# Set-up of a four-layer image kernel: statistics and transposes by image halves, and a new order of its first products

## Chip, cores and metric

The kernel runs on one core of one Trainium2 chip. The metric is the device time of one execution in microseconds; lower is better. A core has TensorE (PE in the profile; PEld is its weight load), VectorE (DVE), ScalarE (ACT), GpSimd (POOL) and SyncE (SP). SP, ACT and POOL also issue DMA transfers, each from a queue of its own, in order.

## What is computed

The input is x, 1024 images of 16 x 16 positions x 16 channels, f32. Four residual blocks follow one another. Each normalises its input by group (mean and variance over two neighbouring channels and all positions of an image, eight groups, with a small number added to the variance), applies a layer, and adds the result to its input. The layers are: a linear map of the whole image (4096 to 4096), given as a tensor train of three cores

```python
for core in cores:
    r, o, i, k = core.shape
    res_t = res.reshape(bs, r, i, -1)
    new = jnp.einsum('roik,brix->bkox', core, res_t)
```

then a cellular-automaton step (a fixed 3 x 3 filter, two dense layers, an alive mask), a 3 x 3 convolution with 16 channels, and a second cellular-automaton step. Only the first block and a piece of weight preparation for the last are touched here.

## The kernel before

The images are worked on as two sets of 512 (n = 0, 1), and each set again as two halves of 256. Images lie in the free dimension, and features in partitions, so x must be transposed: in the file the images are rows.

**The first layer.** The train's cores are multiplied out into a matrix of blocks, and the product of matrix and images is made with a table of 13 products (OUTER) of combined matrix blocks with combined image blocks, and inside each of them with 7 products (INNER, L561) in the manner of Strassen's scheme. A phase is one entry of OUTER; it has 4 units (u, numbered through all phases), each of 7 products of 2 steps. A step is four matmuls of 128 x 128 by 128 x 256 into a half of one PSUM bank (`po`). The phases are run one after the other by `run` (L1987), which calls a phase's steps in order, and between them, at set shares of the phase, the items of background lists: (list, from, to).

Product k of a unit multiplies a matrix (`w11`, `w00`, `w01`, or a sum: `s1`, `s2`, `s5`, `s7`) with a block of images (X[b, t, n]: b half of lines, n image half) or a combination (E[0..2]):

```python
("s2", (0, 0), {(1, 0): 1, (1, 1): -1}),   ("s5", (1, 1), {(0, 1): 1, (0, 0): -1}),
("w11", (1, 0), {(0, 0): 1, (1, 0): 1}),   ("s1", 0, {(0, 0): 1, (1, 1): 1}),
("s7", 1, {(0, 0): 1}),   ("w01", 2, {(1, 1): 1}),   ("w00", (0, 1), {(0, 1): 1, (1, 1): 1}),
```

Around each step `pieces` (L1546) issues work for the same or the next unit: `build` (L1447: 16 or 32 row-tiled matmuls `pw<-R,gq` and four ScalarE copies make a quarter matrix w), `mix` (L1474, VectorE, sums of two blocks of w), `gload` (L1422, loads gq from the DRAM table g_dram), `gather` (L1597, adds po into the unit's result r), and `store` (L1510, writes r into xf in DRAM; where a block has been written before, by an accumulating DMA of POOL at L1541). Engines take their work in the order in which it is issued; a buffer is handed out again when its last reader is done.

**The set-up** (L2041–2092) is written out in order. `train_setup` (L608): `early` (L660) makes 64 products `pg` of two cores, copies them to gw with 16 ScalarE copies (L672), and `keep_g` (L648) writes them to g_dram: four DMAs at L651 to g_dram[0], eight at L658 to g_dram[1]. `rest` is 12 further such pieces (`piece`, L678), which are made in phase 0. `input_steps(0)` (L1063): eight 1 MB loads of x on SP (L1074), `stats` (L1086, bn_stats for 128 images and half their lines), `turn` (L1088, four 128 x 128 transposes and a copy of 512 columns, for one half line, 8 positions x 16 channels, and all 512 images), `aggregate` (L1116), `root` (L1118–1120), `newton` (L1124), `widen` (L1134, means or inverse deviations written out to 128 columns), `spread` (L1142, their transposes, copied into `mr`), `kept` (L1145, lines written to xr in DRAM). `first_normed` (L1176) and `centre_scale` (L1174) subtract the mean and multiply, for the blocks x00, x11, x10, x01 of phase 0; `combined` (L1187, work at L1203) makes the five combinations of blocks; `part_steps(j)` (L1217) makes the image blocks of phase j one phase ahead, which for j = 1 reads xr.

In before, statistics of all 512 images come first, then the first normed block, then phase 0. The half of the transposes that are lines 8–15 (`lines[1]`) run in phase 0 at 0.12–0.42, `part_steps(1)` at 0.43–0.99. The dictionary `before` lists what is issued ahead of which step of phase 0. `set3` (an item list of `nca_weights`, L228) prepares the last layer's weights in phase 7; its `store` (L328–330) writes them to DRAM from POOL, and `conv_weights` and `fold3`, after it, read them or reuse their room in the tile xn.

Of the kernel before, what the change touches and what calls it, by code (L numbers as in the profile page):

```python
# [13 lines left out]
AF = mybir.ActivationFunctionType  # L14
# [91 lines left out]
def conv_preact_kernel(ctx: ExitStack, tc: tile.TileContext, a: dict, out: bass.AP):  # L106
# [483 lines left out]
    def train_setup(room):  # L590
# [57 lines left out]
        def keep_g(h, q, g, queue):  # L648

            for w in range(2):  # L650
                queue.dma_start(  # L651
                    g_dram[0][h, q, w].rearrange("o s k (t f) -> (s k t) o f", t=2),
                    g[64 * w : 64 * w + 64],
                )
            for w in range(2):
                for v in range(2):
                    rows = slice(64 * w + 32 * v, 64 * w + 32 * v + 32)
                    queue.dma_start(  # L658
                        g_dram[1][v, q, w, :, h].rearrange("o k (t f) -> (k t) o f", t=2), g[rows]
                    )  # L660

        def early():

            g = work([P, 2, 8, P], "w0", "gw")
            pg = [bank([P, 2, 4, 64], "w", "pg") for _ in range(4)]
            for x in range(2):
                for k in range(4):
                    for r in range(4):
                        gmul(pg[r][:, x, k], 0, k % 2, x, r, k // 2)
            for q, x, r in product(range(2), range(2), range(4)):  # L670
                f = 64 * x + 16 * r
                A.copy(  # L672
                    g.rearrange("p q (o i) f -> p q i o f", i=2)[:, q, :, :, f : f + S],
                    pg[r][:, x, 2 * q : 2 * q + 2].rearrange("p i (o j) -> p i o j", j=S),
                )
                if (x, r) == (1, 3):
                    keep_g(0, q, g[:, q].rearrange("p (o i) f -> p o (i f)", i=2), G)
# [383 lines left out]
    def input_steps(n, tag, queue):  # L1061
# [4 lines left out]
        slots = flats[1 - n].rearrange("p (s f) -> p s f", s=8)  # L1066
        X = part_lines(0)

        def slot(half, bg):
            return slots[:, 0 if (n, half, bg) == (1, 1, 3) else 4 * half + bg]  # L1070

        def load(half, bg):
            b0 = n * NB + bg * P
            queue.dma_start(  # L1074
                slot(half, bg),
                a["x"][b0 : b0 + P, 8 * half : 8 * half + 8].rearrange("b h w c -> b (h w c)"),
            )
# [10 lines left out]
        def turn(h, wh):  # L1088
            pt = bank([P, 4, P], tag[h % len(tag)], "ptin")
            for bg in range(4):  # L1090
                x = slot(h // 8, bg).rearrange("p (h w f) -> p h w f", h=8, w=2)
                T.transpose(pt[:, bg], x[:, h % 8, wh], ident)
            pt = pt.rearrange("p g b -> p (g b)")
            if n == 0 and h < 8:
                if wh:
                    A.copy(X[:, 1, h], pt)
                else:
                    A.copy(raw[:, h], pt.rearrange("p (n i) -> p n i", n=2))
                return
            if h % 2 == 0:  # L1100
                st["l"] = work([P, 2, NB], "t4", "lines")
            A.copy(st["l"][:, h % 2], pt)
            if h % 2 == 1:
                nc.sync.dma_start(
                    xr[n][wh, h - 1 : h + 1].rearrange("h p b -> p h b"), st["l"]
                )
# [32 lines left out]
        def spread(k):  # L1139
            pt = bank([P, 4, P], tag[0], "ptmr")  # L1140
            for bg in range(4):
                T.transpose(pt[:, bg], st["e", k][:, bg], ident)  # L1142
            A.copy(mr[n][:, k], pt.rearrange("p g b -> p (g b)"))

        def kept(b):  # L1145
            to = xr[n][b, 0:8]
            if b:
                G.dma_start(to.rearrange("h p b -> p h b"), X[:, 1])
                return
            for i in range(2):  # L1150
                G.dma_start(
                    to.rearrange("h p (n b) -> p h n b", n=2)[:, :, i], raw[:, :, i]
                )
# [15 lines left out]
        return loads, stat, lines, tail, [lambda: spread(0), lambda: spread(1)], kept  # L1169
# [6 lines left out]
    def first_normed(b, i):  # L1176

        X, E = part_tile(0)
        cols = slice(256 * i, 256 * i + 256)

        def op(t, k):
            x = X[:, b, t : t + 4, i]
            centre_scale(x, x if b else raw[:, t : t + 4, i], 0, cols, k)

        return [(1.2, lambda t=t, k=k: op(t, k)) for t in (0, 4) for k in range(2)]
# [201 lines left out]
    def layer_train():  # L1387
# [59 lines left out]
        def build(u, h):  # L1447

            if u >= len(units):
                return  # L1450
            R, gs = st["R", units[u][0]], list(st["g", u, h].values())
            w = st["w", u, h] = work([P, 2, 2, 4, P], "w1" if h else "w0", "w")
            pw = [bank([P, 2, 2, P], "w", "pw") for _ in range(4)]
            for v in range(2):
                for i in range(2):
                    for k, g in enumerate(gs):
                        for r in range(4):
                            rows = slice(32 * r, 32 * r + 32)
                            T.matmul(  # L1459
                                pw[r][:, v, i], g[rows, P * (2 * v + i) : P * (2 * v + i) + P], R[rows, k],  # L1460
                                start=k == 0, stop=k == len(gs) - 1,
                            )
            for r in range(4):
                A.copy(  # L1464
                    w.rearrange("p b s t m -> p (b s t) m")[:, :, 32 * r : 32 * r + 32].rearrange(
                        "p k (v o) -> p v k o", v=2
                    ),
                    pw[r].rearrange("p v i (k o) -> p v (i k) o", o=S),
                )
# [4 lines left out]
        def mix(u, what):  # L1474
# [10 lines left out]
            into = block(u, 0, 1)  # L1485
            x, y = block(u, *x), block(u, *y)
            if out:
                t = st[what, u] = work([P, 2, 4, P], out, what)
                V.tensor_tensor(t.rearrange("p s t m -> p (s t m)"), x, y, f)  # L1489
            else:  # L1490
                V.tensor_tensor(into, x, y, f)
# [54 lines left out]
        def pieces(u, k):  # L1546

            ph, q = units[u]
            what, where, goes = INNER[k]

            def go(i):
                X, E = part_tile(ph)
                if i == 0:
                    at = {1: (1, 6144), 3: (1, 14336)}.get(u)
# [9 lines left out]
                po, at = st["po"], 2 * k + i  # L1564
# [3 lines left out]
                if at == 1 and u > 0:  # L1568
                    store(u - 1)
                if at == 2:  # L1570
                    mix(u, "s1")
                if at == 4:
                    mix(u, "s7")
# [6 lines left out]
                if at == 9:  # L1580
                    build(u + 1, 1)
                if at == 11:
                    gload(u + 2, 1)
                if at == 12:
                    mix(u + 1, "s2")
# [4 lines left out]
                if i == 1:  # L1590
                    gather(u, k, po, goes)
# [5 lines left out]
        def gather(u, k, po, goes):  # L1597
            r = st["r", u].rearrange("p s a (n i) -> p s (a n) i", n=2)
            at = {x: 2 * x[0] + x[1] for x in goes}
            if k in (2, 3, 6):  # L1600
# [4 lines left out]
            for x, sign in goes.items():  # L1605
                out = r[:, :, at[x]]
                if all(x not in INNER[j][2] for j in range(k)):
# [6 lines left out]

        steps = [
            [x for u in range(4 * ph, 4 * ph + 4) for k in range(7) for x in pieces(u, k)]
            for ph in range(NP)
        ]
# [421 lines left out]
    with ExitStack() as es:  # L2040
        stage(es, dict(t4=4, s=2, n=2, w1=1, w0=2, s2=1, s5=1, r=1, gq=2, R=2, A=1), dict(w=4, m=1, o=3))  # L2041
        sums, cores, early, rest = train_setup(flats[0][:, 8192:9216])
        tag = ["w"]
        loads, stat, lines, tail, (spread0, spread1), kept = input_steps(0, tag, nc.sync)
        now(loads)
# [3 lines left out]
        now([sums])  # L2049
        coefs(0)  # L2050
        now([cores] + stat[0])
        early()
        gload(0, 1, queue=G)
        gload(0, 0, queue=G)
        now(lines[0])
        kept(0)
        kept(1)
        gload(1, 0)
        gload(1, 1)
        build(0, 1)  # L2060
        build(0, 0)
        now(stat[1] + tail[:2])
        mix(0, "s2")
        now([spread0] + tail[2:] + [spread1])
        x00, x11, x10, x01 = (first_normed(*at) for at in ((0, 0), (1, 1), (1, 0), (0, 1)))
        now(x00[0::2] + x00[1::2])
        mix(0, "s5")
        now(x11[:2])
        tag[0] = "m"
        more = combined(0)  # L2070
        before = {
            1: x11[2:] + rest[0][0:1],
            2: x10 + rest[0][1:2] + more[0:2],
            4: more[2:4],
            5: more[4:6],
            7: x01,
            8: more[6:8],
            9: more[8:10],
        }
        free = (12, 15, 18, 22, 26, 29, 32, 36, 40, 43)  # L2080
        for i, piece in zip(free, rest[0][2:] + rest[1]):
            before[i] = [piece]
# [12 lines left out]
        for j in late:  # L2095
            sums_late(j)
        run(
            steps_of(phases[0]), 107, (), (lines[1], 0.12, 0.42), (part_steps(1), 0.43, 0.99),
        )
        tag.append("w")  # L2100
        loads, stat, lines, tail, more, _ = input_steps(1, tag, G)
# [4 lines left out]
        for i in range(4):  # L2106
# [9 lines left out]
            7: (set3, 0.85),  # L2116
# [85 lines left out]
```

## Time and profile before

| | us |
|---|---|
| median of 3 runs | 2743.33 |
| lowest and highest run | 2742.66, 2747.08 |
| the profiled execution's own time | 2746.07 |
| its span (first to last instruction) | 2744.3 |
| the fourth and the eighth load of x landed | 17.3, 30.6 |
| first product of phase 0 starts | 47.14 |
| last product of phase 0 ends | 182.95 |
| last product of phase 7 ends | 982.8 |

Mean granted TensorE clock: 0.991 of full speed.

How to read the profile: a row of the timeline is a start, a length, an engine, a line, what it writes and reads, how often, and in brackets how long the engine was idle ahead of it and whose work ended that. A row of the windows is a stretch from:to, its length, busy time (and number of instructions) of each engine, the granted TensorE clock, the busy share of the DMA engines and their GB/s. A row of the waits is an engine and what it works on, what it waited for, the total, how often, and the longest. PE busy says that matmuls were under way, not that they ran at full clock. Matmul durations overlap with their neighbours' by a little, so a rate (80 matmul records in 17.46 us) is safer than a mean.

### The profile page before, as it was taken

How to read it: one execution, taken by the hardware profiler on the slowest of the kernel's cores; microseconds unless marked ns; L12 is line 12 of the kernel's file. 1: busy time of each engine (PE TensorE's matmuls, PEld its weight loads, DVE VectorE, ACT ScalarE, POOL GpSimd, SP SyncE). 2: the span in 40 equal slices, each digit the busy share in tenths (PEclk: the TensorE clock that was granted, in tenths of full speed). 3: DMA queues.
4: the chain of work that ended last, by engine and by line, in shares of the span. 5: the costliest groups of instructions: out<-in, count | busy, mean ns of one | idle time of the engine just before them, and what ended most of it. 6: DMA issues, size and time to landing. Idle time of an engine off the chain costs nothing.

```text
span 2744.3 us, 47734 instructions
## 1 busy us (share of the span) xinstructions
PE 2675.8 (98%) x19246; PEld 1756.9 (64%) x19246; DVE 1994.9 (73%) x2416; ACT 1241.4 (45%) x2091; POOL 541.3 (20%) x690
## 2 busy tenths in 40 slices
PE   6999999999999999999999999999999999999997
PEld 5888888888888878888778733333333333334344
DVE  8597667867787766667887777658778858756654
ACT  3324222222232222333332276776767756676664
POOL 2000351312122742311331111111113221110000
PEclk8999999999999999999999999999999999999998
DMA  7686788997897687889689764555575866444665
GB/s 254 215 317 227 242 169 214 236 221 188 193 242 193 154 187 180 226 229 263 171 188 257 148 165 102 108 159 122 106 195 83 202 150 143 101 89 116 180 175 209
DMA packets 264796, 502.17 MB, mean 183 GB/s; under 512 B 32804, under 2 KB 100440, under 8 KB 255360
## 3 DMA queue, kind: packets, MB, share of 16 engines
q1 hardware_dynamic: 180752, 338.78, 37.1%
q0 software_dynamic: 83632, 160.22, 33.9%
q8 instruction: 152, 2.49, 0.4%
q14 instruction: 68, 0.56, 0.1%
q10 hardware_dynamic: 192, 0.13, 0.0%
HBM read 280.66 MB, written 223.35 MB: 184 GB/s over the span
## 4 chain that ended last, share of the span: by engine, by line
PE 81%; DVE 8%; DMA 5%; issue 3%; POOL 1%; ACT 1%; SPq 0%; DVEq 0%; POOLq 0%; ACTq 0%
PE po L1567 37%; PE ph L1974 21%; PE po L1803 8%; PE po L1658 5%; PE pw L1459 4%; DMA xn<-in_x_dram 1%; PE po L1667 1%; DVE xn L1174 1%; DMA xf<-r 1%; DMA xn<-xf 1%; DVE xn L1203 1%; PE ptx L1867 1%; DMA L_conv_kp<-xn 1%; DMA xb<-xn 0%; DMA xn<-xn 0%
## 5 line engine op out<-in xcount | busy, mean ns | idle before, releaser
L1977 ACT ACTIVATE hid<-ph,pack 128x512 f32<-128x512 f32 (+1 forms) x1040 | 641.3, 684 | 313.5 <-PE ph L1974 254.3
L1567 PE MATMUL po<-xn,s 128*128 128x256 f32 x3328 | 756.7, 384 | 13.6 <-DVE s L1489 7.2
L1567 PEld LDWEIGHTS po<-xn,s 128*128 128x128 f32 x3328 | 628.5, 191 | 117.5 <-issue 16.7
L1567 PE MATMUL po<-xn,w 128*128 128x256 f32 x2496 | 565.0, 381 | 1.4 <-DVE xn L1203 1.4
L1974 PE MATMUL ph<-xn,wq 32*128 32x512 f32 (+1 forms) x3752 | 518.3, 590 | 1.9 <-DVE u L1815 1.5
L1567 PEld LDWEIGHTS po<-xn,w 128*128 128x128 f32 x2496 | 468.2, 190 | 74.1 <-issue 5.9
L1464 ACT COPY w<-pw 128x512 f32<-128x512 f32 x416 | 213.6, 600 | 454.6 <-PE pw L1459 371.8
L1974 PEld LDWEIGHTS ph<-xn,wq 32*128 32x128 f32 x3752 | 233.6, 184 | 228.9 <-issue 210.0
L1974 PE MATMUL ph<-xn,pack 32*128 32x512 f32 x1288 | 274.2, 607 | 5.6 <-DVE u L1815 1.6
L1489 DVE TENSOR_TENSOR s<-w 128x1024 f32<-128x1024 f32 x208 | 251.2, 1217 | 28.1 <-PE po L1567 24.8
L1803 PE MATMUL po<-hid,pack 128*32 128x512 f32 (+1 forms) x2080 | 256.0, 592 | 0.8 <-ACT hid L1977 0.5
L1815 DVE SCALAR_TENSOR_TENSOR u<-po,pack,xn 128x512 f32<-128x512 f32 (+1 forms) x130 | 96.3, 741 | 168.2 <-PE po L1803 167.1
L1857 POOL DMA_DIRECT2D xf<-u x96 | 82.6, 860 | 618.7 <-DVE u L1855 592.1
L754 DVE TENSOR_TENSOR xn<-xn,m 128x1024 f32<-128x1024 f32 x128 | 150.2, 1217 | 34.7 <-ACT m L777 34.6
L1974 PEld LDWEIGHTS ph<-xn,pack 32*128 32x128 f32 x1288 | 115.6, 184 | 90.7 <-issue 63.1
L1803 PEld LDWEIGHTS po<-hid,pack 128*32 128x32 f32 x2080 | 53.9, 109 | 174.9 <-ACT hid L1977 86.3
L1658 PE MATMUL po<-xn,convw 128*128 128x512 f32 x368 | 163.6, 598 | 0.0
L1203 DVE TENSOR_TENSOR xn<-xn 128x1024 f32<-128x1024 f32 x130 | 152.7, 1215 | 8.0 <-DMA L_conv_kp<-xn 8.0
L1459 PE MATMUL pw<-R,gq 32*128 32x128 f32 x3328 | 143.7, 286 | 7.5 <-DVE small L1116 6.9
L1603 DVE TENSOR_TENSOR r<-r,po 128x1024 f32<-128x1024 f32 x78 | 95.0, 1218 | 72.9 <-PE po L1567 61.0
L1459 PEld LDWEIGHTS pw<-R,gq 32*128 32x128 f32 x3328 | 116.2, 188 | 41.9 <-issue 38.6
L1541 POOL DMA_DIRECT2D xf<-xn x69 | 89.8, 1776 | 251.2 <-DVE xn L1534 71.7
(229 smaller groups left out, 2784.9 us busy)
## 6 DMA issues: line engine op xcount, KB each, us to landing
xn<-xf SPq DMA_DIRECT2D x128, 512.0 KB
xn<-xb SPq DMA_DIRECT2D x36, 1024.0 KB
wq<-L_conv_wy SPq DMA_DIRECT2D x192, 192.0 KB
xf<-xn POOLq DMA_DIRECT2D x69, 512.0 KB, 10.8
piece<-xb SPq DMA_DIRECT2D x64, 512.0 KB
xf<-r POOLq DMA_DIRECT2D x48, 512.0 KB, 12.7
xf<-u POOLq DMA_DIRECT2D x96, 256.0 KB, 4.2
gq<-g_dram SPq DMA_DIRECT2D x94, 256.0 KB
```

The lines of the kernel that those rows point to most:

```text
L754: V.tensor_tensor(part, part, m().unsqueeze(1).broadcast_to([P, 2, NB]), op)
L1203: V.tensor_tensor(out, y, z, f)
L1459: T.matmul(pw[r][:, v, i], g[rows, P * (2 * v + i) : P * (2 * v + i) + P], R[rows, k], start=k == 0, stop=k == len(gs) - 1,)
L1464: A.copy(w.rearrange("p b s t m -> p (b s t) m")[:, :, 32 * r : 32 * r + 32].rearrange("p k (v o) -> p v k o", v=2), pw[r].rearrange("p v ...
L1489: V.tensor_tensor(t.rearrange("p s t m -> p (s t m)"), x, y, f)
L1567: T.matmul(po[:, i], matrix(u, what)[:, i, t], x, start=t == 0, stop=t == 3)
L1603: V.tensor_tensor(part, part, po.unsqueeze(2).broadcast_to([P, 2, 2, 256]), ALU.add)
L1658: T.matmul(st["po", h][wh], conv["fw"][:, y], X[:, 16 * wh + h + y - 1], start=y == max(0, 1 - h), stop=y == min(2, S - h),)
L1803: T.matmul(po[32 * j : 32 * j + 32], nca["w1"][:, v], hid[j], start=v == 0, stop=v == 1)
L1815: V.scalar_tensor_tensor(u, po, nca["b1"], X[:, 8 * q + w2, cols(hf)], ALU.add, ALU.add)
L1974: T.matmul(ph, w, x, start=k == 0, stop=k == len(tiles) - 1)
L1977: A.activation(h, ph, AF.Relu, bias=nca["bt"][:, r : r + 1])
```

## The change

- **Loads and statistics by halves.** `first_images` takes the place of `input_steps(0)`. SP loads images 0–255 (four loads of 1 MB); the other four loads are issued from POOL, two after the first g_dram writes and gq loads, two after the second g_dram writes. Statistics, root, Newton step, widening and spreading are done for 256 images at a time. A `turn` now takes two half lines of 256 images, again four transposes and one copy; its PSUM banks alternate between two tags.
- **The transposes.** In the set-up: all lines of images 0–255. In phase 0: all lines of images 256–511, in groups of 16 ahead of steps 4, 6 and 8. Their number is the same.
- **`early`** issues the copies and the g_dram[0] writes of q = 0 first, then `gload(0, 1)` and `gload(0, 0)`, then q = 1; the g_dram[1] writes come last on POOL.
- **Order of phase 0.** Products s2 and w11 of units 0 and 1, which need only images 0–255, come first; then the others. `build(1, 1)` and `mix(1, "s2")` move ahead, into other rooms; `gather` asks which results have been made rather than for fixed numbers.
- **Work ahead of the steps** (`before`): statistics of images 256–511, their root, widening and spreading, x11 and two pieces stand ahead of step 8, the first that needs them; x01 ahead of step 12.
- **Background of phase 0:** no `lines[1]`; `part_steps(1)` at 0.3–0.99 (0.43–0.99 before).
- **`set3`** in phase 7 ends at 0.75 of it (0.85 before).

```diff
-        loads, stat, lines, tail, (spread0, spread1), kept = input_steps(0, tag, nc.sync)
-        now(loads)
+        load, stats, turns, aggregate, root, newton, widen, spread = first_images(tag)
+        for bg in range(2):
+            load(0, bg)
+            load(1, bg)
...
-        now([cores] + stat[0])
-        early()
-        gload(0, 1, queue=G)
-        gload(0, 0, queue=G)
-        now(lines[0])
...
+        def first_g():
+            gload(0, 1, queue=G)
+            gload(0, 0, queue=G)
+            load(0, 2, G)
+            load(1, 2, G)
+
+        early((first_g, lambda: (load(0, 3, G), load(1, 3, G))))
+        stats(0, 1)
+        stats(1, 1)
+        aggregate(0)
+        aggregate(1)
+        now(turns(0, 0, 0))
+        root(0)
+        widen(0, 0)
+        newton(0)
+        widen(1, 0)
+        spread(0, 0)
+        part = turns(0, 0, 1)
+        now(part[:2])
+        spread(1, 0)
+        now(part[2:])
...
+        now(x00[0::2] + x00[1::2])
         build(0, 1)
         build(0, 0)
+        gload(1, 1)
+        gload(1, 0)
+        now(x10[0::2])
         mix(0, "s2")
+        now(x10[1::2] + more[0:2])
+        now(turns(1, 0, 0) + turns(1, 0, 1))
+        half1 = turns(1, 1, 0) + turns(1, 1, 1)
+        rest = rest[0] + rest[1]
         before = {
-            1: x11[2:] + rest[0][0:1],
-            2: x10 + rest[0][1:2] + more[0:2],
-            4: more[2:4],
-            5: more[4:6],
-            7: x01,
-            8: more[6:8],
-            9: more[8:10],
+            2: [lambda: build(1, 1)],
+            3: [lambda: stats(0, 2), lambda: mix(1, "s2")],
+            4: turns(0, 1, 0),
+            5: [lambda: stats(1, 2)],
+            6: turns(0, 1, 1),
+            7: [lambda: stats(0, 3), lambda: mix(0, "s5")],
+            8: [lambda: stats(1, 3), lambda: aggregate(2), lambda: aggregate(3)]
+            + half1[:4] + [lambda: root(1), lambda: widen(0, 1)]
+            + [lambda: newton(1), lambda: widen(1, 1), lambda: spread(0, 1), lambda: spread(1, 1)]
+            + rest[:2] + half1[4:] + x11[0::2] + x11[1::2],
+            9: more[2:4],
+            11: more[4:6],
+            12: x01[0::2] + x01[1::2],
+            13: more[6:8] + rest[2:3],
+            15: more[8:10] + rest[3:4],
         }
...
+            if ph == 0:
+                us = [(0, 0), (0, 2), (1, 0), (1, 2)] + [x for x in us if x[0] > 1 or x[1] not in (0, 2)]
...
-            steps_of(phases[0]), 107, (), (lines[1], 0.12, 0.42), (part_steps(1), 0.43, 0.99),
-        )
+        run(steps_of(phases[0]), 107, (), (part_steps(1), 0.3, 0.99))
...
-            7: (set3, 0.85),
+            7: (set3, 0.75),
```

The new routines, cut to what differs:

```python
def turn(half, i, wh, h):
    tag.append(tag.pop(0))
    pt = bank([P, 2, 2, P], tag[0], "ptin")
    for l, g in product(range(2), range(2)):
        x = slot(half, 2 * i + g).rearrange("p (h w f) -> p h w f", h=8, w=2)
        T.transpose(pt[:, l, g], x[:, h + l, wh], ident)
...
def root(i):
    gs = slice(2 * i, 2 * i + 2)
    V.tensor_scalar(st["ve"][:, gs], st["mv"][:, gs, :, 1], GN_EPS, None, ALU.add)
    A.activation(st["t"][:, gs], st["ve"][:, gs], AF.Sqrt)
...
def keep_g(h, q, g, queue, first=True, second=True):
    for w in range(2 * first):
        queue.dma_start(g_dram[0][h, q, w]...)
```

## Prediction

> **What bounds the kernel now.** I read the page's busy shares first, then the busy time of each engine by stretch (set-up, phase 0, the boundary to phase 1), then the timeline of the set-up, the clock in single 3.3 us stretches, and the waits around the two places where TensorE stands still.
>
> ```profile
> span 2744.3 us, 47734 instructions
> ...
> PE 2675.8 (98%) x19246; PEld 1756.9 (64%) x19246; DVE 1994.9 (73%) x2416; ACT 1241.4 (45%) x2091; POOL 541.3 (20%) x690
> ```
>
> TensorE is busy for 98%, so only its idle time (68 us) and its time at half clock can be won. By stretch (start:end, length, then busy time of PE, PEld, DVE, ACT, POOL, clock, DMA share, GB/s):
>
> ```profile
> 0.00:47.14 47.14, 24.17 (x211) 21.71 (x211) 37.13 (x143) 19.71 (x49) 15.37 (x30) 0.81 0.91 342
> 47.14:182.95 135.81, 134.16 (x960) 112.63 (x960) 104.53 (x97) 43.33 (x112) 0.56 (x1) 0.96 0.64 213
> 182.95:190.00 7.05, 4.25 (x13) 3.44 (x13) 7.05 (x7) 0.00 (x0) 3.16 (x6) 0.76 1.02 312
> ```
>
> The set-up holds a third of all idle time: 23 of 47 us. Phase 0 has none to speak of. At its end TensorE stands 2.8 us while VectorE is busy through the whole stretch. The set-up's path is seen in the timeline (start, length, engine, line, what, [idle before <- releaser]):
>
> ```profile
> 30.60 2.71 DVE L1086 BATCH_NORM_STATS2 bn<-xn 128x6 f32<-128x256 f32 x8
> 33.67 2.09 PE L1459 MATMUL pw<-R,gq 32*128 32x128 f32 x32 [6.89 <-DVE small L1116]
> 43.05 0.63 DVE L1134 COPY wide<-small 128x128 f32<-128x128 f32 x4
> 43.60 4.62 DVE L1174 TENSOR_TENSOR xn<-xn 128x1024 f32<-128x1024 f32 x4
> 47.14 3.78 PE L1567 MATMUL po<-xn,s 128*128 128x256 f32 x8 [2.63 <-DVE xn L1174]
> ```
>
> The last 1 MB of x lands at 30.6, its statistics follow, then root, Newton step, spreading and the first normed block: 16.5 us from landing to the first product. The clock (PE busy, clock, DMA share, GB/s):
>
> ```profile
> 29.50:32.80 3.30, 0.00 (x0) 0.50 0.91 332
> 46.60:49.90 3.30, 2.76 (x7) 0.50 0.04 14
> 50.00:53.30 3.30, 3.30 (x20) 0.50 0.00 0
> 53.40:56.70 3.30, 3.30 (x10) 0.50 0.00 0
> 56.80:60.20 3.40, 3.40 (x28) 1.00 0.08 18
> 183.10:186.40 3.30, 0.65 (x3) 1.00 1.04 288
> 186.50:189.90 3.40, 3.40 (x10) 0.50 0.99 330
> ```
>
> The idle set-up costs twice: the products from 47.1 to 56.8 run at half clock, 9.6 us for 4.8 us of work. The boundary wait does the same to 186.5–189.9: 1.7 us. Last, phase 8, where set3's weight stores are in the way:
>
> ```profile
> DVE xn L1203 <- DMA L_conv_kp<-xn: 8.0, 1, 8.0
> ACT xn L1609 <- DMA xf<-xn: 16.1, 1, 16.1
> ```
>
> **Part 1, the first product comes earlier.** Images 0–255 need four of the eight loads; in before the fourth landed at 17.3. Their last statistics then end near 20.3 (8 of them 2.7, with a short queue). Two aggregates of 0.69 to 21.7, root 0.3, half a widening 0.3, Newton 1.3, half a widening 0.3: 24.0, against 43.7 in before. The first normed block (4 x 1.16) is done at 28.7. So statistics are no longer late; the block matrices are. The first eight copies of gw follow half the products, so the first two g_dram writes are issued about 2 us before the 15.17 of before. There they took 8.6 us and more beside the x loads; now the loads are in by 17.3, so I put their landing at 20, and that of the gq load, 4.2 us in before, at 24.5. In before it was queued behind all writes, on GpSimd, until 29.03. From there the steps of before count (pw 2.1 cold, four copies, the second build, the mix 1.2): 32.9 for the second build. After it TensorE's order has 32 transposes for lines 8–15, which ScalarE empties in eight copies: 7.4 us at the cold 0.85 per four. First product at 40.2, so **6.9 us earlier**. Bounds: 36 if the transposes are warm, 47 if the gq load is as late as now. The half-clock products go too, since transposes fill the two windows ahead; I keep 0.5 of the 4.8, **4.3 less**.
>
> Queues: the eight g_dram[1] writes go last on GpSimd, behind four loads, but the first pair of lines that reads them, (0,1), comes in phase 2. The xr writes go from GpSimd (37.4–47.9 in before) to SP behind unit 1's gq loads, at some 0.6 each; only part_steps(1) reads them, from 0.30 of the phase on. Bounds 0 to 1; I take nothing.
>
> A page of the Trainium skill speaks against another piece: "DMA: Bandwidth & Descriptors", Issuing engines are not separate DMA queues, says that transfers from any engine end on the same 16 DMA engines. The g_dram writes that took 8.6–12.4 us beside loads at 420 GB/s, against 2.5–3.7 later alone, agree; by the page the four loads on GpSimd's queue win nothing by themselves, and their gain here is only that they start behind the gq loads.
>
> **Part 2, phase 0's own work** does not change: 56 steps of 1.746 (80 matmul records in 17.46), 8 builds of 1.1, 12 pieces of 1.1, 64 transposes at 0.6 per four: 129.4 us, which is before's 135.81 without 1.65 idle and 4.8 half clock. Half the transposes are still in the phase, those of images 256–511.
>
> **Part 3, two new waits.** The first four products (steps 0–7: 14.0, with a build and 32 transposes, 5.9, among them) last to about 60.8. In the whole phase I add 1.8 for pieces that take up to 1.24 and for transposes that wait for one of two banks. Then every further product needs x11 or x01, and these need statistics that are started only here: on VectorE behind the last gather 0.65, eight bn_stats 2.65, aggregates 1.4, root 0.3 and ScalarE's square root 0.3, widening 0.3, Newton 1.3, and x11's four operations 4.6: 11.7 us with the short waits between. Behind it in TensorE's queue stand 32 transposes, two pieces and small ones, 6.1 us. The wait is thus 6.0 us warm; but 4.5 of it lie in one piece, more than the 2.80 that made the clock half at 183, and the pieces ran in 1.97 instead of 1.1 and the transposes at 0.85 instead of 0.44 per four when cold, so I add 3.1: **9.1 us**. Bounds: 6.0 (no cold window) and 19 (rival 2). The second wait is ahead of the product of (0,5): VectorE has x01 (4.6), two more sums, mixes s7 and w01 and a gather in front, I count **2.9** (0 to 5).
>
> The page "TensorE: Matmul & The Clock Gate", Part 1, What's actually happening, has full speed back after one busy window of about 3.4 us. Products ran without a gap from 47.14 and were half until 56.8, with a run of sixteen 16-row matmuls in the window 50.0–53.3, so the row gives longer than the page; an estimate by the page puts the cold part at 1.7 instead of 3.1.
>
> Sum of phase 0: 40.2 + 0.5 + 129.4 + 1.8 + 9.1 + 2.9 = 183.9, against 182.95. Phase 0 ends **1.0 later**: what the set-up wins, the middle gives back.
>
> **Part 4, the boundary.** The second half of phase 0 held, in VectorE, 28.7 us per unit of 26.6 us: that is why it is busy from 136 to 185.75 but for 4 us, and the mix s is late. With part_steps(1) over 0.30–0.99 instead of 0.43–0.99, its share (about 18 of the 28.7) falls by 0.81, to 25.3 per unit. So the 2.8 idle and 1.7 half clock, **4.5 less**. Bounds: 0 (its gathers come behind x01's work, and VectorE is still behind) and 4.5. The line transposes that were spread over 0.12–0.42 are gone from there, so this stretch is lighter for TensorE as well, and nothing else is late.
>
> **Part 5, set3 at 0.75.** The store L328–L330 goes ahead of the unit's accumulating writes instead of behind them. In before kp was issued at 980.7 and landed at 998.2, and L1203 waited 8.0; TensorE stood 2.5 + 0.8 + 0.4 + 0.6. Earlier it lands near 986, before its reader (989). But those writes then queue behind L328, which waits for copies landing about 974, and land near 997 instead of 993.8; ScalarE's copy into that buffer already waited 16.1 for them, and TensorE follows. I take 4.3 won and 2.8 given back, **1.5 less**; bounds 4 more and 5 less.
>
> Sum: +1.0 (phase 0) - 4.5 - 1.5 = -5.0. Against the profiled execution's 2746.07 (span 2744.3) that is 2741.1. This execution lay 2.7 above the median of the runs, so I forecast 2743.33 - 5.0 = 2738.3. About 0.2% (5.5 us) is what a measurement of this kernel can tell from no change, so the forecast lies on the edge of "the same": 2737.8 is the bound.
>
> **Rivals.**
> 1. *The wait in the middle stays warm or set3's stall goes wholly.* The 4.5 us idle may be split over two windows (2.37 in one piece at 1364 made the clock half, 2.53 at 997 did not). Then 3.1 or 2.8 or both come back: 2733 to 2735. For it: the transposes lie in the first part of the wait. Against it: 2.80 was enough at 183.
> 2. *Slower: the clock stays half after the wait.* Steps 8 to 17 run with pieces and VectorE waits among them, as the window 50.0–53.3 did, and no window is filled with wide matmuls until about 101. Eight steps (14), a build and two pieces at half clock cost 13 more less the 2.9 that the second wait then hides: +10.3, 2748.6, and up to 2752. It decides where the first full window after the wait is cold beyond 75. Against it: from 52.75 on a window of products alone set it free.
> 3. *Nothing is won at the ends.* The gq load is late behind x loads, so the first product starts past 43, or VectorE is as far behind at the boundary and 4.5 stays: 2742 to 2746. For it: VectorE gets statistics and x11 into phase 0 that were in the set-up. Against it: up to 136 VectorE had room, with 27 us idle at waits for products, where it now works.
>
> **How the numbers follow.** Forecast 0.50 (2736 to 2742), rival 1 0.22, rival 2 0.10, rival 3 0.18. A little under half of the forecast's own case and nearly all of rival 1 lie below 2737.8: faster 0.45. Rival 2's upper part and a little of rival 3 lie above 2748.8: slower 0.09. The rest, 0.46, is the same. The range takes in rival 1's better end and rival 3, with rival 2's lower part left out: 2731 to 2747.
>
> **What would show it.** The first product of L1567 near 40; the second widening of images 0–255 ended near 24; no half clock in the first products; a stretch near 61–73 with a half clock and TensorE released by VectorE's wide and x11 operations; a wait of some 3 us ahead of (0,5) near 90–100; phase 0's last product near 184 and no wait behind it; kp landing near 986 without a VectorE wait, and ScalarE's wait for xf<-xn ending near 997. It is wrong if the first product starts later than 43, if the middle wait passes 12, or if VectorE is busy without a gap over the boundary.

## The result, and the profile after

The changed kernel takes 2751.72 us (median of 10 runs, 2749.01 to 2757.93) against 2743.45 (10 runs, 2741.40 to 2751.22): ratio 1.0029, 95% interval 1.0020 to 1.0039. It is slower by 8 us, where 5 us faster was forecast. The profiled execution took 2749.45 (span 2747.7), in the lower part of its runs, and that of before 2746.07, in the upper part of its own; so the two traces are only 3.4 us apart, and the experiments have to say which of the waits vary. One execution of a_xract, below, ran at a granted clock of 0.847 throughout (3088.77 us); its ratio leaves it out, and its row of phase 0 is from a second profile.

The page's first lines of after: the same number of matmuls, and TensorE's share is the same but for rounding (97.5% in both).

```profile
span 2747.7 us, 47757 instructions
...
PE 2678.5 (97%) x19246; PEld 1759.4 (64%) x19246; DVE 1995.6 (73%) x2424; ACT 1242.3 (45%) x2094; POOL 527.4 (19%) x691
```

Set-up, phase 0 in four parts, and the first 7 us of phase 1:

```profile
0.00:38.32 38.32, 25.35 (x207) 21.57 (x208) 34.48 (x105) 18.76 (x48) 14.37 (x30) 0.91 0.86 313
38.32:63.86 25.54, 20.91 (x132) 17.69 (x131) 8.64 (x21) 9.74 (x19) 0.55 (x1) 0.93 0.67 227
63.86:76.00 12.14, 7.52 (x61) 6.36 (x58) 11.26 (x40) 5.60 (x17) 0.00 (x0) 0.76 0.36 122
76.00:100.00 24.00, 19.42 (x112) 15.53 (x111) 16.41 (x16) 5.21 (x13) 0.00 (x0) 0.84 0.35 99
100.00:193.00 93.00, 91.69 (x674) 77.06 (x673) 75.13 (x73) 24.21 (x69) 1.17 (x3) 1.00 0.79 263
193.00:200.00 7.00, 7.00 (x34) 6.17 (x33) 7.00 (x7) 2.09 (x4) 2.55 (x5) 1.00 1.01 387
```

The first product starts at 38.32, 8.8 us earlier. But the next 62 us hold 14 us of TensorE idle time (4.6 + 4.6 + 4.6), where before had 1.65 in all of phase 0, and they run in part at half clock (0.93, 0.76, 0.84). The waits, from TensorE's own timeline:

```profile
45.49 1.40 PE L1546 MATMUL pw<-R,gq 32*128 32x128 f32 x32 [3.55 <-DMA gq<-g_dram]
46.82 5.13 PE L1660 MATMUL po<-xn,w 128*128 128x256 f32 x16
...
69.41 0.46 PE L1157 MATMUL ptmr<-ident,wide 128*128 128x128 f32 x2 [3.29 <-DVE wide L1149]
70.91 0.69 PE L1157 MATMUL ptmr<-ident,wide 128*128 128x128 f32 x2 [1.04 <-DVE wide L1149]
71.53 2.89 PE L644 MATMUL pg<-cores,convw 16*128 16x64 f32 x32
74.36 3.80 PE L1102 MATMUL ptin<-ident,xn 128*128 128x128 f32 x16
77.95 4.85 PE L1660 MATMUL po<-xn,s 128*128 128x256 f32 x16
...
90.76 3.62 PE L1660 MATMUL po<-xn,s 128*128 128x256 f32 x8 [3.21 <-DVE xn L1286]
...
98.70 1.99 PE L1660 MATMUL po<-xn,w 128*128 128x256 f32 x8 [1.37 <-DVE xn L1286]
```

Each matmul of a product stands in the trace as two records, so eight records are a step and sixteen a product. Counted from 38.32, the wait at 45.49 is ahead of product (0,2) (unit 0, product 2), those at 69.41 and 70.91 ahead of (0,1), that at 90.76 ahead of (0,4), which needs the combination E[1] (E1 below), and that at 98.70 ahead of (0,5), which needs E[2].

Read the lengths beside the waits. Sixteen records take 3.62 us at full clock; behind the first wait they take 5.13, behind the second 4.85, and behind the third eight take 3.62 instead of 1.99. Each of these three waits is paid a second time in clock: 1.5, 1.2 and 1.6 us, and the pieces and transposes at 71.5 to 78 on top. The clock in single stretches (PE busy, clock, DMA share, GB/s):

```profile
67.00:70.40 3.40, 0.46 (x2) 0.97 0.72 249
70.40:73.80 3.40, 2.89 (x32) 0.50 0.00 0
73.80:77.20 3.40, 3.40 (x19) 0.50 0.15 33
77.20:80.60 3.40, 3.40 (x12) 0.53 0.94 244
80.60:84.00 3.40, 3.40 (x44) 1.00 1.02 317
```

Where the span went, by the end of each phase on TensorE (after less before): phase 0 ends 9.1 us later (192.0 against 183.0), phase 1 at +9.0, phase 6 at +8.8, phase 8 at +5.4, the span at +3.4. So the boundary to phase 1 gave nothing, set3 in phases 7 and 8 gave 3.4, and 2.0 more fell in later phases, which the change doesn't touch; from the end of phase 8 on the kernels below scatter by 4 us.

At the boundary the wait for `s` is gone, but at 206.82 TensorE waits 2.83 for the fourth load of images 512–1023, with a half clock behind it:

```profile
206.82 0.48 PE L1192 MATMUL ptin<-ident,xn 128*128 128x128 f32 x1 [2.83 <-DMA xn<-in_x_dram]
207.09 3.40 PE L1660 MATMUL po<-xn,s 128*128 128x256 f32 x8
```

### The profile page after: what moved, and what is told of

It is laid out like the page before. It is cut to its first block, busy times and chain, and to the rows that moved or that the text cites. A ratio compares the mean times of both kernels' runs of the same rounds, so it can differ in the third digit from the quotient of the medians.

```text
span 2747.7 us, 47757 instructions
## 1 busy us (share of the span) xinstructions
PE 2678.5 (97%) x19246; PEld 1759.4 (64%) x19246; DVE 1995.6 (73%) x2424; ACT 1242.3 (45%) x2094; POOL 527.4 (19%) x691
## 4 chain that ended last, share of the span: by engine, by line
PE 85%; DVE 7%; DMA 3%; issue 1%; ACT 1%; SPq 0%; POOL 0%; DVEq 0%; POOLq 0%; ACTq 0%
PE po L1660 41%; PE ph L2070 21%; PE po L1899 8%; PE po L1754 5%; PE pw L1546 5%; PE po L1763 1%; DMA xn<-xf 1%; DMA xn<-in_x_dram 1%; PE ptx L1963 1%; PE ptin L1192 1%; DVE u L1911 1%; DVE xn L1286 0%; PE pcnt L1939 0%; DMA xn<-in_L_conv_fc_w_dram 0%; DVE xn L757 0%
## 5 line engine op out<-in xcount | busy, mean ns | idle before, releaser
L1660 PE MATMUL po<-xn,s 128*128 128x256 f32 x3312 | 748.9, 383 | 8.3 <-DVE s L1579 5.1
## 6 DMA issues: line engine op xcount, KB each, us to landing
wq<-L_conv_wy SPq DMA_DIRECT2D x192, 192.0 KB
```

The source lines that it names most:

```text
L1660: T.matmul(po[:, i], matrix(u, what)[:, i, t], x, start=t == 0, stop=t == 3)
```

## The experiments

Medians and ratios against before, which ran beside each (2742.79 to 2744.45 in the three sets of runs); phase 0's first product and end from the profile (a_xract's from its second profile). After did not run beside the experiments, so a difference to its median can be off by about 1.5 us; the ratios are the safer comparison.

| kernel | median us | ratio, 95% | phase 0 |
|---|---|---|---|
| before | 2743.45 | | 47.1–183.0 |
| after | 2751.72 | 1.0029, 1.0020–1.0039 | 38.3–192.0 |
| b_set3 | 2743.14 | 0.9995, 0.9986–1.0004 | 47.0–184.5 |
| b_parts | 2742.84 | 0.9996, 0.9987–1.0005 | 47.1–183.9 |
| a_loads | 2753.05 | 1.0034, 1.0021–1.0047 | 38.0–195.7 |
| a_stats | 2745.52 | 1.0007, 0.9998–1.0016 | 36.8–188.5 |
| a_actq | 2748.41 | 1.0012, 1.0002–1.0021 | 41.7–194.0 |
| a_late1 | 2750.82 | 1.0025, 1.0015–1.0034 | 36.5–197.6 |
| a_stats_actq | 2741.30 | 0.9985, 0.9975–0.9995 | 42.0–184.2 |
| a_best | 2736.45 | 0.9965, 0.9953–0.9978 | 40.7–179.9 |
| a_xract | 2745.40 | 1.0006, 0.9997–1.0015 | 38.8–188.6 |
| a_best2 | 2731.19 | 0.9953, 0.9939–0.9967 | 38.0–175.4 |
| b_best | 2740.98 | 0.9992, 0.9982–1.0001 | 47.3–186.7 |

Theory A, from the profile of after: the loss is order, not work; unit 1's gq load is late, the chain of statistics starts too late, and the boundary's stall had covered another wait. The main rival: VectorE's work binds the first 100 us, and removing one wait only moves it.

**b_set3, set3 alone.**

```diff
-            7: (set3, 0.85),
+            7: (set3, 0.75),
```

> The kernel before with one number changed: set3 ends at 0.75 of phase 7 instead of 0.85. Theory A (the earlier store of L_conv_kp takes the 8.0 us VectorE wait out of phase 8 and nothing gives it back): phase 8 about 5 us shorter, phase 7 up to 2 us longer because its PE work on fc_w meets a load, in all 3 us faster than before, about 2740. Theory B (as forecast: the accumulating xf writes behind L328 land later and ScalarE's copy waits for them): phase 8 only 1.5 us shorter.

In the profile phase 8 is 5.1 shorter and phase 7 1.5 longer (a 1.39 us wait at L287, fc_w's transposes, which now come before their load), as theory A has it. L_conv_kp lands at 971.5, 972.4, well before its reader, and the accumulating writes at 974.7 to 981.5, earlier too: the whole list of set3 was moved up, not its last item alone, so nothing was given back. The timed runs show only 1.3 less, and the interval includes none and 3.8. The next experiment gives a likely reason.

**b_parts, the boundary alone.**

```diff
-            steps_of(phases[0]), 107, (), (lines[1], 0.12, 0.42), (part_steps(1), 0.43, 0.99),
+            steps_of(phases[0]), 107, (), (lines[1], 0.02, 0.29), (part_steps(1), 0.3, 0.99),
```

> The kernel before with lines 8-15 transposed at 0.02-0.29 of phase 0 and part_steps(1) at 0.30-0.99 (0.12-0.42 and 0.43-0.99 before). Theory A (the 2.8 us wait for s at the start of phase 1 hides a wait for the x loads of images 512-1023, which can start only when phase 0's buffers are free): the wait for s goes, a wait of 2 to 3 us for xn<-in_x_dram with a half clock after it comes in its place some 10 us later, 0 +- 1.5 us against before. Theory B (the forecast's): 2.8 idle and 1.7 at half clock go, 4.5 us faster.

Theory A held in where, less in how much. The wait for `s` at phase 1's start is gone, and TensorE waits here instead:

```profile
195.28 0.55 PE L1092 MATMUL ptin<-ident,xn 128*128 128x128 f32 x3
198.71 0.33 PE L1092 MATMUL ptin<-ident,xn 128*128 128x128 f32 x1 [2.88 <-DMA xn<-in_x_dram]
198.88 1.90 PE L1567 MATMUL po<-xn,s 128*128 128x256 f32 x8
```

The three transposes done and the fourth waiting are one group: it needs 128 images from each of four loads. The loads were issued from 182.46, when VectorE's last read of their room was done, and the fourth landed at 198.67. The eight matmuls behind it took 1.90: no half clock this time, and phase 1 is 1.9 shorter than before's. The median is 1.6 below before's, with an interval that includes none. In the same run phase 8 is 3.7 shorter although set3 was left alone: kp landed at 993.8 instead of 998.2, and VectorE waited 4.3 for it instead of 8.0. Phases 7 and 8 together took 220.5 us here without set3's edit and 220.5 in b_set3 with it, against 224.2 in the profile of before. So that profile caught the stall at a length that another trace doesn't show, and what the edit is worth in the median is not shown to differ from nothing.

**a_loads, GpSimd's loads of x behind the g_dram[0] writes.**

```diff
         def first_g():
             gload(0, 1, queue=G)
             gload(0, 0, queue=G)
-            load(0, 2, G)
-            load(1, 2, G)
 
-        early((first_g, lambda: (load(0, 3, G), load(1, 3, G))))
+        early((first_g, lambda: [load(half, bg, G) for bg in (2, 3) for half in range(2)]))
```

> The changed kernel with the four loads of images 256-511 behind the second pair of g_dram[0] writes on GpSimd's queue (two of them were ahead of it). Theory A (those writes land at 33.2 behind the loads, so the gq load of unit 1 starts at 33.3 and lands at 45.5 beside the loads): the gq load starts near 28 and lands before 42, the 3.55 us wait of L1546 and the half clock after it go, 4 to 5 us faster than the changed kernel. Theory B (the lateness is the bandwidth and goes to the loads instead): statistics of images 256-511 come later, the wait ahead of step 8 grows by as much, no change.

Theory A missed. B's "no change" came in time (1.0034 against 1.0029), but not for its reason: the wait ahead of step 8 was the same 3.29 and 1.04 us. g_dram[0] landed at 28.3, 5 us earlier, SP issued the first gq load at 28.35, and it landed later than in after. SP's queue, then TensorE:

```profile
19.51 7.36 SPq L1115 DMA_DIRECT2D xr<-xn  x2
28.35 3.70 SPq L1521 DMA_DIRECT2D gq<-g_dram  x2
```

```profile
48.67 2.09 PE L1546 MATMUL pw<-R,gq 32*128 32x128 f32 x32 [7.02 <-DMA gq<-g_dram]
```

A 256 KB load took 20 us, more than the 12.2 in after (33.29 to 45.5). Ahead of it in the same queue are two xr writes of 1 MB each, in rows of 1 KB, the second issued 1.9 us before it: the writes that the change moved from GpSimd's queue to SP's. That gave theory A2, order within SP's queue.

**a_stats, statistics of images 256–511 ahead of step 3.**

```diff
-            3: [lambda: stats(0, 2), lambda: mix(1, "s2")],
+            3: [lambda: stats(0, 2), lambda: stats(1, 2), lambda: stats(0, 3), lambda: stats(1, 3)]
+            + [lambda: aggregate(2), lambda: aggregate(3), lambda: root(1), lambda: widen(0, 1)]
+            + [lambda: mix(1, "s2"), lambda: newton(1), lambda: widen(1, 1)],
             4: turns(0, 1, 0),
-            5: [lambda: stats(1, 2)],
-            6: turns(0, 1, 1),
-            7: [lambda: stats(0, 3), lambda: mix(0, "s5")],
-            8: [lambda: stats(1, 3), lambda: aggregate(2), lambda: aggregate(3)]
-            + half1[:4] + [lambda: root(1), lambda: widen(0, 1)]
-            + [lambda: newton(1), lambda: widen(1, 1), lambda: spread(0, 1), lambda: spread(1, 1)]
-            + rest[:2] + half1[4:] + x11[0::2] + x11[1::2],
+            6: [lambda: spread(0, 1), lambda: spread(1, 1)] + turns(0, 1, 1),
+            7: [lambda: mix(0, "s5")],
+            8: x11[0::2] + x11[1::2] + half1[:4] + rest[:2] + half1[4:],
```

> The changed kernel with all statistics of images 256-511 up to the second widening ahead of step 3, their spreading ahead of step 6, x11 first in front of step 8. Theory A (the wait in the middle is the chain from bn_stats to mr that starts only at step 7's end): idle 3.3 + 1.0 us and the half clock from 70 to 80 go, about 8 us faster than the changed kernel. Theory B (VectorE's sum of work binds the first 100 us, and its order only decides where the wait is): the wait moves to steps 3 to 5 or to x01 ahead of step 12, at most 3 us faster.

6 us faster than after by the medians; in the profile steps 7 to 8 shrink from 14.1 us (63.86 to 77.95) to 6.4 (67.01 to 73.38), and the clock stays full there:

```profile
47.20 2.09 PE L1546 MATMUL pw<-R,gq 32*128 32x128 f32 x32 [6.80 <-DMA gq<-g_dram]
...
69.20 1.94 PE L644 MATMUL pg<-cores,convw 16*128 16x64 f32 x32
71.07 1.09 PE L1102 MATMUL ptin<-ident,xn 128*128 128x128 f32 x8
72.45 1.09 PE L1102 MATMUL ptin<-ident,xn 128*128 128x128 f32 x8 [0.28 <-ACT lines L1109]
73.38 2.97 PE L1660 MATMUL po<-xn,s 128*128 128x256 f32 x13
```

So the wait in the middle was the late start of the chain, and worth 7.7 us there: VectorE had room at 39 to 49. Part of it is lost again in the wait for gq, 6.80 in this run.

**a_actq, unit 1's gq loads on ScalarE's queue.**

```diff
-        gload(1, 1)
-        gload(1, 0)
+        gload(1, 1, queue=A)
+        gload(1, 0, queue=A)
```

> The changed kernel with the two gq loads of unit 1 on ScalarE's queue instead of SP's. In the run with the loads of x moved back these two were issued 5 us earlier, at 28.4 and 31.7, and PE still waited until 48.7. Theory A2 (they stand behind the two 1 MB xr writes, in rows of 1 KB, that the change put on SP's queue): on a queue of their own they land some 5 us after issue near 34, and the 3.55 us wait and the half clock after it go, 5 us faster than the changed kernel. Theory B (the DMA engines as a whole are full until 46, whatever queue): they land near 45 as before, no change.

A2 held: issued at 35.04, no earlier than in after, they were there when TensorE came at 45.26, without a wait and without a half clock: step 2 starts 4.7 us after step 0, in after 8.5. TensorE came late enough that its timeline alone can't tell A2 from B; the semaphores in the trace can: the first load landed at 41.8, 6.8 us after its issue, where B had it near 45. The gain of 3.3 us is below the 5 expected, because ScalarE's queue stood at the issue until g_dram landed (31.96 to 35.04); the engine was idle for 2.32 us ahead of its next copies, the half clock lasted to 41.5, and the first product came at 41.7.

**a_late1, the transposes of images 512–1023 later.**

```diff
-            steps_of(phases[1]), 107, (), ([(0, x) for x in loads[:7]] + [8] + woven_in + tail, 0.0, 0.76),
+            steps_of(phases[1]), 107, (), ([(0, x) for x in loads[:7]] + [14] + woven_in + tail, 0.0, 0.76),
```

> The changed kernel with the transposes of images 512-1023 begun 14 instead of 8 us into phase 1. Theory A (what is late at the boundary, once the wait for s is gone, is the fourth 1 MB load, which lands 3.4 us after its first transpose is due): the 2.83 us wait and the half clock after it go, 4 us faster than the changed kernel. Theory B: the wait comes back at the next group of transposes or as VectorE load at the end of phase 1, no change.

The wait and the half clock are gone and phase 1 is 2.9 shorter than before's (after: 0.1), so in the profile theory A held, at 2.8 instead of 4. The median moved by 0.9 only, inside the intervals, so the timed runs don't show the gain by themselves. This kernel's phase 0 is the same code as after's, and so a second sample of it: the wait for gq was 6.15 here instead of 3.55, and phase 0 ended at 197.6 instead of 192.0. After's own profile has the shortest of the four such waits in kernels that leave writes and loads on SP's queue (3.55, 6.15, 6.80, 7.02).

**a_stats_actq, both edits.**

> The changed kernel with both edits: all statistics of images 256-511 ahead of step 3, and unit 1's gq loads on ScalarE's queue. If A2 holds the two gains add, since the early statistics alone only made the wait for gq longer (6.8 instead of 3.55): phase 0 ends near 181 to 183, 5 us ahead of the run with early statistics alone. If B holds: as that run, 2745.5. If VectorE's order binds after that, the wait shows up ahead of (1,2) or at x01.

2741.30: the gains add, 10.4 us below after, and the kernel is now slightly faster than before (ratio 0.9985, interval to 0.9995). Phase 0 ends at 184.2, 4.3 ahead of a_stats. The rival, by which a removed wait only comes back, is left only with the 3.21 us at 81.10, the wait for E1.

**a_best: also x01 ahead of step 7 and the later transposes of phase 1.**

```diff
-            7: [lambda: mix(0, "s5")],
+            7: [lambda: mix(0, "s5")] + x01[0::2] + x01[1::2],
...
-            12: x01[0::2] + x01[1::2],
...
-            steps_of(phases[1]), 107, (), ([(0, x) for x in loads[:7]] + [8] + woven_in + tail, 0.0, 0.76),
+            steps_of(phases[1]), 107, (), ([(0, x) for x in loads[:7]] + [14] + woven_in + tail, 0.0, 0.76),
```

> Early statistics, unit 1's gq loads on ScalarE's queue, x01 ahead of step 7 (VectorE stood 10 us there in the run with early statistics), and the transposes of images 512-1023 begun 14 us into phase 1. By theory A with A2 the four waits of phase 0 and the one of phase 1 go: 5 for gq, 8 for the statistics, 6 for x01, 4 for the boundary, less 2 for a phase that VectorE then binds: some 15 to 20 us below the changed kernel, 2733 to 2736, faster than both. If VectorE's sum of work binds (rival), not below 2743.

2736.45, 15.3 below after, faster than both kernels and half a microsecond short of the expected range. Phase 0 ends at 179.9; the 3.21 us for E1 are still there, at 79.99.

**a_xract, the two xr writes on ScalarE's queue.** This undoes the suspected part and leaves the gq loads where they were.

```diff
-            nc.sync.dma_start(to.rearrange("h p b -> p h b"), x)
+            (A if h + i == 0 else nc.sync).dma_start(to.rearrange("h p b -> p h b"), x)
```

> The changed kernel with the two 1 MB xr writes of images 0-255, lines 0-7, on ScalarE's queue; the gq loads of unit 1 stay on SP's. This undoes the part of the change that put these writes ahead of the loads in one queue. Theory A2 (order within SP's queue): gq lands some 5 us after its issue at 33 to 35, the wait of L1546 and its half clock go, and the first product keeps its early start near 37 to 38, 4 to 6 us faster than the changed kernel. Rival (ScalarE's queue is served faster than SP's, whatever stands in it; the gain of the last such run was the queue): gq on SP is as late as before, no change.

> The same kernel as the last but one experiment (xr writes of lines 0-7 on ScalarE's queue), for a profile at full clock, the first one's clock having been 0.85 throughout. Theory A2: no wait of L1546 for gq, steps 0 to 7 in 22 us instead of 25.5, phase 0 ends 4 to 6 us earlier than the changed kernel's. Rival: the wait is there and the time came from elsewhere.

6.3 us below after by the medians; A2 held, and the rival, that ScalarE's queue is the faster one, fell. The profile shows SP's gq load issued at 34.55 (by its semaphore it landed at 41.5, 6.9 us later) and no wait:

```profile
38.79 3.62 PE L1660 MATMUL po<-xn,s 128*128 128x256 f32 x16
42.34 1.17 PE L1546 MATMUL pw<-R,gq 32*128 32x128 f32 x32
43.44 3.72 PE L1660 MATMUL po<-xn,w 128*128 128x256 f32 x16
```

Steps 0 to 7 took 20.3 us (38.8 to 59.1) against 25.5 in after. Phase 0 ends 3.4 us earlier than after's, less than the 4 to 6 expected: the half clock at the wait for E1 lasts from 84.5 to 94.8 here, in after from 90.7 to 94.1. The DMA packets in the traces show the order itself: in after the gq load's first packet moved at 41.5, 8.2 us after its issue and behind 1874 packets of 1 KB of the same queue; here at 38.1, 3.5 us after its issue, with none of them ahead in its queue.

**a_best2, a_best with the xr writes moved instead of the gq loads, and E1 earlier.**

```diff
-            9: more[2:4],
-            11: more[4:6],
+            9: more[2:6],
```

> Early statistics, x01 ahead of step 7, transposes of images 512-1023 14 us into phase 1, as in the fastest run so far; but with the xr writes on ScalarE's queue in place of the gq loads, and with the third combination E1 issued two steps earlier (the 3.2 us wait at 80.0 was for it). By theory A with A2: first product 3 to 4 us earlier than 40.7, the wait at 80 gone, 4 to 6 us faster than 2736.5. Rival (VectorE binds): the wait shows up behind it, no change.

2731.19, the fastest: 20.5 us below after, 12 below before (ratio 0.9953). Its gq load, issued at 35.10, ended a wait of 0.92 at 42.5, so it took about 7.4 us. Ahead of (0,4) TensorE waits 0.82, now for a mix, instead of 3.21 for E1, with no half clock behind it. No run tells the two edits' shares of the 5.3 us below a_best apart.

**b_best, the edits beside the set-up, on before.** part_steps and lines as in b_parts, set3 as in b_set3, [14] as in a_late1.

> The kernel before, its set-up as it was, with three edits: lines 8-15 at 0.02-0.29 and part_steps(1) from 0.30, the transposes of images 512-1023 begun 14 us into phase 1, set3 to 0.75. By theory A the wait for s and the one for the x loads are both gone (4 us), and the wait for L_conv_kp (3 us): 2737 to 2740, which is what the changes beside the set-up are worth. Rival (nothing is won at the boundary, the wait moves on): 2742.

2740.98: 1 us short of what was expected, and the interval (0.9982 to 1.0001) just includes no change. The profile has, against that of before, phase 1 3.1 shorter and phases 7 and 8 3.6, but phase 0 3.6 longer, with a wait of 2.28 at 149.3 that before did not have. By the medians of b_best and a_best2, the set-up by halves, with its waits gone and E1 earlier, is worth about 10 us.

## Why the prediction was wrong

**The first product** was right in kind: statistics ended at 23.6 (24.0 forecast), the block matrices were late after them, and the first product started at 38.3, 1.9 earlier than the 40.2 of the sum.

**The step that failed first is the one on the queues:** "The xr writes go from GpSimd (37.4–47.9 in before) to SP behind unit 1's gq loads ... Bounds 0 to 1; I take nothing." They went ahead of these loads: SP issued the two of 1 MB at 18.54 and 26.89, the first load at 33.29:

```profile
18.54 8.72 SPq L1115 DMA_DIRECT2D xr<-xn  x2
33.29 0.83 SPq L1521 DMA_DIRECT2D gq<-g_dram  x2
```

The code says so (`turns(0, 0, ...)` ends in `kept`, and the loads come after both), and I had it the other way round. It cost 3.55 us of wait and 1.5 of half clock in the profile, 5.0 in all, and more in other runs; a_actq and a_xract take it away from either side. The Trainium skill bears on it, in "DMA: Bandwidth & Descriptors", Two DMAs through the same engine are not ordered: within one queue of one DMA engine, descriptors start in order, though they need not finish so. The runs agree, in so far as the first gq load took 11 to 20 us behind the writes (after, a_stats, a_late1, a_loads) and 6.8 to 7.4 without them (a_actq, a_xract, a_best2). The section that the prediction cited, by which transfers from any engine share the same 16 DMA engines, is no reason to leave the queue's order out.

**The wait in the middle** was forecast as 9.1 and the products as in effect 15.2 behind the end of step 7; they were 15.3 behind. That the two agree so closely is in part luck: the idle time was 4.6 (0.29, 3.29 and 1.04), not 6.0, and the work at half clock, with the first product, took 4.6 more than its price at full clock, not 3.1. (The 6.0 is also 0.4 more than 11.7 less 6.1.) What the forecast did not ask is whether the change had to start the chain there; a_stats shows that it had not.

**The wait ahead of (0,5)** was forecast at 2.9 and was 1.4. The 3.2 us that look like it stand one product earlier, ahead of (0,4), where the forecast had nothing, and they were paid twice, with 1.6 of half clock behind them. That is a third step that failed, and the likeness of the two numbers is chance. TensorE waited there for E1, and VectorE had been idle for 7.55 us just before:

```profile
86.49 0.69 DVE L1706 TENSOR_TENSOR r<-r,po 128x512 f32<-128x512 f32 x1 [7.55 <-ACT r L1702]
...
89.49 2.35 DVE L1286 TENSOR_TENSOR xn<-xn 128x1024 f32<-128x1024 f32 x2
```

E1 was issued ahead of step 11, behind a gather that waits for TensorE's and ScalarE's work on (0,1) and two mixes; a_best2 issues it two steps earlier, and E1 is no longer waited for. So this wait too was order, not VectorE's sum of work. Together the two waits took 6.2, 3.3 more than the 2.9. Against the sum of 183.9: -1.9 (first product) + 5.0 (queue) + 0.1 (middle) + 3.3 + 1.6 = 8.1, which gives 192.0; the 1.6 are what is left, smaller waits of the rest of the phase that were not traced one by one.

**The boundary** is the second step that failed: "the 2.8 idle and 1.7 half clock, 4.5 less ... nothing else is late." The loads of the next 512 images were late, 2.83 and a half clock; phase 1 is 0.1 shorter. The trace of before showed these loads issued from 181.5 to 187.7, landing from 189 on, the fourth at 198.9: their transposes waited for nothing only because the stall ahead had put them off. Reading when the next late thing arrives would have shown it. Rival 3 had "VectorE is as far behind"; the size was its, the cause was not.

**set3** was forecast at 1.5 and gave 3.4 between the profiles. The term that was mis-sized is "2.8 given back": none was. But the stall that it removes was longer in the profile of before than in that of b_parts (8.0 against 4.3), and b_set3's median is 1.3 below before with an interval that includes none; that 1.3 lies near the 1.5 is luck.

**The rivals.** Rival 2, a clock that stays half to 101, did not come: a stretch of transposes and products, from 77.0 to 80.4, set it free. The case that came, slower by waits on a queue and on loads, was in no rival; rival 3 was the nearest, and it had these only as "late behind x loads" and for the start of the first product. The range, 2731 to 2747, reached from a little below rival 1 to just above rival 3, and no bound of the queue step was above 1.

## What to carry to other kernels

When a change moves a DMA to another queue, write down the new queue in order with times, and look at what stands behind the moved transfer: here a 256 KB load that TensorE needed soon came 4 to 13 us later for standing behind two writes of 1 MB. Ahead of crediting a removed stall, find the next arrival at that point in the trace (here a load that landed 3 us later), since the stall may have been covering it. Match a wait to the product it delays before comparing it with a forecast. And price a wait of 2 to 3 us as an either-or: once idle, or once more at half clock, by where it falls, as the next section shows.

## What the runs showed of the hardware that was not expected

A 256 KB load behind two 1 MB writes in 1 KB rows on the same queue, while all queues together moved some 370 GB/s, took 11 to 20 us; issuing it 5 us earlier, right behind the second write (a_loads), made it land 3 us later. Why it was later is open, and so is whether the length of the rows matters: no run varies it.

The half clock follows idle time within fixed stretches, not the length of a wait. In the traces of the 13 kernels in the table the clock changes only at points that lie whole multiples of 3.41 us apart (in after 46.3, 49.7, 70.2, 80.4, 90.7, 94.1, 206.7, 210.1). Cut by these points, from 40 us to the end of the first layer, every stretch at full clock with 2.0 us or more of TensorE idle time was followed by one at half clock, and those with less were not, but for two: 1.88 us in 142.3–145.7 of b_parts, and 0.29 in 61.4–64.9 of a_best2, a stretch filled with transposes and pieces. So the 2.83 us at the boundary of after (2.72 of idle time within 203.3–206.7) halved the clock, while the 2.88 of b_parts fell into two stretches with 1.06 and 1.82 and left it full, and so did the 3.21 of a_stats at 84.97 (1.5 and 1.7). The kernel can't choose where the points fall: in after they lie 0.5 us from where they lie in a_stats.
